# Perceiver block on one core: deviations of the projections' heads, centring of the keys' weights, scaling of inputs, and gathering of the lanes' maxima

## The chip, the cores and the metric

The kernel runs on one core of a Trainium2 chip. The metric is device time in microseconds (us) of one execution, and the median over runs is compared. The engines that matter are TensorE (PE: matmuls and transposes; PEld: its weight loads), VectorE (DVE), ScalarE (ACT), GpSimd (POOL), and the DMA queue of SyncE (SP), on which all transfers are issued. Each engine works through its own instruction list in order and waits for others by semaphores.

## The reference

A perceiver block, in float32, on x (128 x 512) and a context of 12,544 tokens of 512 channels. What matters for the change:

```python
def _ln(x, w, b):            # over the last axis
    mu = jnp.mean(x, -1); var = jnp.mean((x - mu)**2, -1)
    return (x - mu) * rsqrt(var + EPS) * w + b
def _div_clamp_fp8(x, scale):
    y = clip(x / scale, -448, 448)
    return fp8_roundtrip(bfloat16(y))
def _fp8_linear(x, wq, w_scale, in_scale):
    return (_div_clamp_fp8(x, in_scale) * in_scale) @ wq.T * w_scale
```

- x is normalised per row (`_ln`, the kernel does it twice in one), then four fp8-rounded projections give 16 query heads for the context (wqx), 8 key heads (wk), 8 value heads (wv) and 16 query heads for self-attention (wq), all of 128 channels, each with its own per-channel in_scale. The heads of wqx, wk and wq are layer-normalised per head.
- Self-attention over the 128 rows, and cross-attention of the same rows over the keys and values that w_kv_x makes from the context; its keys are layer-normalised per head too. Two heads of queries share a head of keys. Both results are fp8-rounded, projected and added to x.
- A causal 16-head attention with its projections, and a mixture of 32 experts of which each row takes 8.

## The kernel before, in words

**Stages.** (1) Norm of x, and twelve projections of 512 columns, each with 1 MB of weights; (2) self-attention in four groups of four heads; (3) cross-attention over 25 chunks of the context, 24 of 512 tokens and, as number 12 in the middle, one of 256 (the half chunk); (4) the causal attention and the experts.

**First stage (main loop L518 to L568).** `begin(name)` issues the four matmuls of a projection (shown as eight in the trace, ps_p, L462); weights come from a ring of three tiles w, and each begin loads the next. Projections run three ahead of their ends. `end(i)` (L477) normalises the four heads of projection i: `norm_heads` (L146) takes statistics on DVE (L152, L154), makes the variance plus eps (L156), its power of -1/2 (L158) and the weights' scale (L159) on POOL and minus mean times that, nb4b, on DVE (L161); ACT then writes the normalised pnn in four instructions (L163). PE turns pnn around (ps_t, L222), and ACT applies gain and bias (L474). Projections 6 and 7, the values, take one ACT copy instead. `quantised` (L444) divides the normalised x by in_scale (L192, four instructions of 128x128), rounds it (L198: a bfloat16 clip, a mask and additions) and multiplies by in_scale again (L448, four instructions); it runs once for each of the four projection kinds, on DVE.

**Keys and values of the context.** Each pair of key heads or of token blocks is made by a seven-product scheme (`unit`, L289; `k_unit` L321, `v_unit` L341): sums of weight blocks (`mix_weights`, wsum and wkv) and of context blocks (`mix_tokens`, L267 to L270, mix and ctx) are multiplied into three PSUM tiles a_ps, b_ps and c_ps, which DVE and ACT combine into KT and V through the copies p1, u2, u3 (u, L299). The keys' weights are first centred per head: a row sum on DVE (wm, L554), its scaling (L555), and its addition on POOL (L557), for eight blocks. In the first stage the units of chunk 0 fill PE between projections.

**A chunk.** `scores` (L639) multiplies KT with the queries and evicts with krs (the keys' 1/deviation, from `k_sums`, and from `k_rstd` with its matmul v_ps, kve and a power on POOL, L384); DVE takes block maxima mxr (L658). `max_rows` (L666) turns these into running maxima for two pairs of key heads at a time: a maximum over the chunk's token blocks (L673, 128 lanes), four copies of 32 lanes each into one tile of 32 lanes (L680), four reduces from it back to the four groups of 32 lanes (L686), and small additions (L691 to L699). `spread` (L713) subtracts the maximum (L725, DVE), exponentiates (L729, ACT), scales the running sums ol by al (L731, POOL) and adds the probabilities' sums to them (L739, POOL). `outputs` (L742) multiplies with V and adds to ol (L752). The loop over key heads g (L798 to L825) runs the values' units; the loop `keys` (L395) makes the keys of the next chunk between the outputs.

**Order.** The order on each engine is fixed when the program is built, by a scheduler that simulates durations; `tc.issue_after(x)` holds instructions back until x has been placed, and `tc.high_priority()` prefers them. So an edit can move neighbours. The lines that the change touches are in `norm_heads`, `norm_rows`, `quantise`, `quantised`, `end`, the main loop, `keys`, `max_rows` and the chunk loop.

Of the kernel before, what the change touches and what calls it, by code (L numbers as in the profile page):

```python
# [45 lines left out]
def block_kernel(  # L46
# [60 lines left out]
    nc.gpsimd.memset(ones, 1.0)  # L107

    fold = keep.tile([P, 32], F32, name="fold")
    nc.vector.tensor_tensor(fold, ident[:, 0:32], ident[:, 32:64], ALU.add)  # L110
    nc.vector.tensor_tensor(fold, fold, ident[:, 64:96], ALU.add)
    nc.vector.tensor_tensor(fold, fold, ident[:, 96:128], ALU.add)
    nc.vector.tensor_scalar(fold, fold, 1.0 / D, None, ALU.mult)
    rcol = keep.tile([P, NCOL], F32, name="rcol")
    c0 = _COLS["q_in"][0]
    nc.vector.reciprocal(rcol[:, c0 : c0 + 16], colt[:, c0 : c0 + 16])
    c1 = _COLS["smooth"][0]
    nc.vector.reciprocal(rcol[:, c1 : c1 + 32], colt[:, c1 : c1 + 32])

    qxT = keep.tile([P, NH, S], F32, name="qxT")  # L120

    qb = keep.tile([P, NH, 4], F32, name="qb")
    ps2 = keep.tile([P, 1], F32, name="ps2")
    nc.vector.tensor_tensor(ps2, scl("pin"), scl("pw"), ALU.mult)
    sc2 = keep.tile([P, 6], F32, name="sc2")
    nc.vector.tensor_tensor(sc2, sc, sc, ALU.mult)

# [18 lines left out]
    def norm_heads(dst, src, sname):  # L146


        st = small.tile([P, 4, 6], F32, tag="st4", name="st4")
        mv = small.tile([P, 4, 2], F32, tag="mv4", name="mv4")  # L150
        for j in range(4):
            nc.vector.bn_stats(st[:, j, :], src[:, j * D : (j + 1) * D])  # L152
        for j in range(4):
            nc.vector.bn_aggr(mv[:, j, :], st[:, j, :])  # L154
        v = small.tile([P, 4], F32, tag="ve4", name="ve4")
        nc.gpsimd.tensor_scalar(v, mv[:, :, 1], sc2[:, scn(sname)], EPS, ALU.mult, ALU.add)  # L156
        r = small.tile([P, 4], F32, tag="rs4", name="rs4")
        nc.gpsimd.tensor_tensor(r, v, mhalf[:, :4], ALU.pow)  # L158
        pool = nc.gpsimd.tensor_scalar(r, r, scl(sname), None, ALU.mult)  # L159
        b = small.tile([P, 4], F32, tag="nb4b", name="nb4b")  # L160
        dve = nc.vector.scalar_tensor_tensor(b, mv[:, :, 0], -1.0, r, ALU.mult, ALU.mult)  # L161
        for j in range(4):
            nc.scalar.activation(  # L163
                dst[:, j * D : (j + 1) * D], src[:, j * D : (j + 1) * D], AF.Identity,
                bias=b[:, j : j + 1], scale=r[:, j : j + 1],
            )
        return pool.ins, dve.ins

    def norm_rows(dst, src, twice=False):

        st = small.tile([P, 6], F32, tag="st1", name="st1")
        mv = small.tile([P, 2], F32, tag="mv1", name="mv1")
        nc.vector.bn_stats(st, src)
        nc.vector.bn_aggr(mv, st)


        v = small.tile([P, 1], F32, tag="ve1", name="ve1")
        if twice:
            nc.gpsimd.tensor_scalar(v, mv[:, 1:2], 1.0 + EPS, EPS * EPS, ALU.mult, ALU.add)
        else:  # L180
            nc.gpsimd.tensor_scalar(v, mv[:, 1:2], EPS, None, ALU.add)
        rs = small.tile([P, 1], F32, tag="rs1", name="rs1")
        nc.gpsimd.tensor_tensor(rs, v, mhalf[:, :1], ALU.pow)
        nc.vector.tensor_scalar(dst, src, mv[:, 0:1], rs, ALU.subtract, ALU.mult)

    def quantise(pool, dst, src, rname, k0):


        r0 = _COLS[rname][0] + k0
        t = pool.tile([P, 4, S], F32, tag="qz_t", name="qz_t")  # L190
        for k in range(4):
            nc.vector.tensor_scalar(  # L192
                t[:, k, :], src[:, k, :], rcol[:, r0 + k : r0 + k + 1], FP8_MAX,
                ALU.mult, ALU.min,
            )
        rounded(pool, dst, [t])
# [39 lines left out]
    V = vp.tile([P, CH // P, G * D], F32, name="V")  # L236
    rstds = {}

# [156 lines left out]
    def keys(c, others, pool, tag, todo=None, done=0):  # L395

        sums = {}
        todo = todo or parts(k_unit(c, u) for u in range(2))
        for i in range(done, 8):
            next(todo)  # L400
            if i % 4 == 3:
                sums[i // 4] = k_sums(c, i // 4)
            if others:
                others(i)
            if i == 6:
                k_rstd(c, 0, sums.pop(0), pool, tag)
        return sums

    with tc.tile_pool(name="pre", bufs=2) as pre, tc.tile_pool(name="pre1", bufs=1) as pre1, tc.tile_pool(
# [25 lines left out]
        xn = pre.tile([S, H], F32, tag="xn", name="xn", bufs=1)  # L435
        norm_rows(xn, x1c, twice=True)
        ps = transposed(pps, xn)
# [6 lines left out]
        def quantised(nm):  # L444
            t = pre.tile([P, NK, S], F32, tag="xq", name=f"x_{nm}")
            quantise(pre, t, lnT, nm, 0)
            for k in range(NK):
                end = nc.vector.tensor_scalar(t[:, k, :], t[:, k, :], col(nm, k), None, ALU.mult)  # L448
            return t, end.ins
# [17 lines left out]

        def end_norm(i, sname, wname, bname, dstT):
            ps = begun[i][0]
            n = pre.tile([S, H], F32, tag="pnn", name="pnn")  # L470
            last = norm_heads(n, ps, sname)
            with tc.issue_after(begun[i + 2][1]) if i + 2 < len(begun) else nullcontext():
                pt = transposed(pps, n)
            nc.scalar.activation(dstT, pt, AF.Identity, bias=col(bname), scale=col(wname))  # L474
            return last

        def end(i):  # L477
            if i < 4:


                qraw = pre.tile([P, 4, S], F32, tag="qT", name="qraw", bufs=4)
                last = end_norm(i, "wqx", "qxln_w", "qxln_b", qraw)
                nc.vector.tensor_scalar(
                    qxT[:, 4 * i : 4 * i + 4, :], qraw, col("kxln_w"), None, ALU.mult
                )
                qraws.append(qraw)
                return last
            if i < 6:
                return end_norm(i, "wk", "kln_w", "kln_b", kT[:, 4 * i - 16 : 4 * i - 12, :])
            if i < 8:  # L490
                nc.scalar.activation(
                    vv[:, (i - 6) * H : (i - 5) * H], begun[i][0], AF.Copy, scale=scl("wv")
                )
                return None
            qTs.append(pre.tile([P, 4, S], F32, tag="qT", name="qT", bufs=4))
            return end_norm(i, "wq", "qln_w", "qln_b", qTs[-1])

# [20 lines left out]
        for i in range(12):  # L518
# [15 lines left out]
            if i == 5:  # L534
                with tc.issue_after(begun[8][1]):
                    for h in range(NH):
# [3 lines left out]
                        )  # L540
                qbw = pre1.tile([32, NH, 4], F32, name="qbw")
                for k in range(4):
                    nc.vector.tensor_copy(qbw[:, :, k], psb[32 * k : 32 * k + 32])
                for b in range(4):
                    nc.vector.tensor_copy(qb[32 * b : 32 * b + 32], qbw)
            if i in (2, 6):
# [3 lines left out]

            for j in {3: (0,), 4: (1,), 5: range(2, 8)}.get(i, ()):
                wk = wkv[:, j % 4, j // 4, :H].rearrange("p (g d) -> p g d", g=4)
                wm = small.tile([P, 4], F32, tag="wm", name="wm", bufs=8)
                nc.vector.tensor_reduce(wm, wk, AX.X, ALU.add)  # L554
                nc.vector.tensor_scalar(wm, wm, -1.0 / D, None, ALU.mult)  # L555
                with tc.issue_after(pooled):
                    nc.gpsimd.tensor_tensor(  # L557
                        wk, wk, wm[:, :, None].to_broadcast([P, 4, D]), ALU.add
                    )
            if i == 7:  # L560
                for k in range(2):
                    for step in mix_weights(nc.vector, slice(0, H), k):
                        step()
            if i == 8:
                first_keys = parts(k_unit(0, u) for u in range(2))
                with tc.issue_after(begun[11][1]):
                    next(first_keys)
        made = pooled  # L568

        def weights_of(i):  # L570
# [24 lines left out]
        def heads_of(i, pe):  # L595
# [15 lines left out]
            for k in range(4):  # L611
                nc.tensor.matmul(psx, lhsT=cq[:, k, :], rhs=w[:, k, :], start=k == 0, stop=k == 3)  # L612
            load_ahead()
# [52 lines left out]
    def max_rows(c, j0, n):  # L666
# [4 lines left out]
        g0 = j0 % 2 * 2  # L671
        r = tmp.tile([P, 4, HS // 32], F32, tag="mx2", name="mx2")[:, : 2 * n, :]
        nc.vector.tensor_reduce(  # L673
            r, mxr[j0 // 2][:, g0 : g0 + 2 * n, :nt, :].rearrange("p g t k -> p g k t"),
            AX.X, ALU.max,
        )

        w = tmp.tile([32, 4, 32], F32, tag="mx4", name="mx4")[:, :, : 16 * n]
        for b in range(4):
            nc.vector.tensor_copy(  # L680
                w[:, b, :], r[32 * b : 32 * b + 32].rearrange("p g k -> p (g k)")
            )
# [115 lines left out]
    for c in range(NCH):  # L798
# [4 lines left out]
        for g in range(G):  # L803
# [10 lines left out]
            if g == 2 and c + 1 < NCH:  # L814
                with tc.issue_after(made):
                    for step in mix_tokens(c + 1):
# [379 lines left out]
```

## Time and profile before

| | us |
|---|---|
| median of 3 runs (lowest, highest) | 2197.46 (2194.74, 2199.66) |
| the profiled execution's own time | 2197.58 |
| its span | 2195.8 |
| PE busy | 2158.6 (98%) |
| DVE, POOL, ACT busy | 1298.3, 1075.0, 900.3 |
| mean granted PE clock | 0.995 |
| L680, four copies: one copy min / median / max | 0.159 / 0.169 / 1.214 |
| L384 krs, mean of one | 2.859 |
| L731, L739 on POOL, mean of one | 1.280, 0.732 |

The span starts with the first and ends with the last recorded instruction; the execution's own time adds what lies around it (1.8 us). In the rows of a timeline the columns are the start, the busy length, engine, line, operation, output and inputs, shapes and how many instructions the row joins; in brackets stand the idle time ahead of it and what ended that. In the rows by stage the busy time of PE, PEld, DVE, ACT and POOL follow the stage's length, each with its number of instructions, and then the granted PE clock, the busy share of the DMA and GB/s. A wait's row gives the total, how often, and the longest.

### The profile page before, as it was taken

The page shows a single profiled execution, that of the slowest core. Times are in us where ns is not written, and L with a number is a line of the kernel's source. Part 1 is how long each engine was busy: PE and PEld are TensorE (multiplying, and loading weights), DVE is VectorE, ACT ScalarE, POOL GpSimd, SP SyncE. Part 2 cuts the span into 40 slices and gives each one's busy share as a digit, 9 for nine tenths or more (in the row PEclk, how much of TensorE's full clock was granted, in tenths as well). Part 3 has the DMA queues.
Part 4 walks back from the last instruction along what each step waited for, and adds up shares of the span by engine and source line. Part 5 has one row for each costly group of instructions (what it writes and reads, how often), then busy time and mean ns, then how long its engine had stood idle before and what let it go on. Part 6 is the DMA issues. An engine that isn't in the chain of part 4 may idle for free.

```text
span 2195.8 us, 23886 instructions
## 1 busy us (share of the span) xinstructions
PE 2158.6 (98%) x8700; PEld 1539.2 (70%) x8700; DVE 1298.3 (59%) x2410; ACT 900.3 (41%) x1686; POOL 1075.0 (49%) x1165
## 2 busy tenths in 40 slices
PE   7999999999999999999899999999999999999999
PEld 3667767766776777677667776776777677676654
DVE  7565764675566457557675576567556646757311
ACT  2443444454345444434354344345434444541211
POOL 2314644764564466457554574475457447534000
PEclk9999999999999999999999999999999999999999
DMA  8300000000000000000000000000000000007593
GB/s 296 124 26 1 20 20 1 20 20 0 20 20 20 1 20 20 0 10 20 20 20 0 20 20 20 1 19 20 1 20 19 20 1 20 0 1 264 192 284 118
DMA packets 71221, 95.48 MB, mean 43 GB/s; under 512 B 3136, under 2 KB 39488, under 8 KB 71104
## 3 DMA queue, kind: packets, MB, share of 16 engines
q1 hardware_dynamic: 71104, 93.97, 13.0%
q8 instruction: 68, 1.11, 0.2%
q14 instruction: 49, 0.40, 0.1%
HBM read 93.69 MB, written 0.26 MB: 43 GB/s over the span
## 4 chain that ended last, share of the span: by engine, by line
PE 91%; DVE 5%; POOL 2%; ACT 1%; issue 1%; SPq 0%; DMA 0%; POOLq 0%; ACTq 0%; DVEq 0%
PE a_ps L329 15%; PE o_ps L747 15%; PE s_ps L647 14%; PE a_ps L348 14%; PE c_ps L329 7%; PE c_ps L348 7%; PE gu_ps L1111 4%; PE b_ps L348 4%; PE b_ps L329 4%; PE moe_acc L1132 2%; PE ps_p L462 1%; PE ps_proj L857 1%; PE ps_core L612 1%; POOL ol L739 1%; DVE mxr L658 1%
## 5 line engine op out<-in xcount | busy, mean ns | idle before, releaser
L739 POOL TENSOR_TENSOR ol<-ol,s 128x256 f32<-128x256 f32 x764 | 553.1, 732 | 31.2
L652 ACT ACTIVATE s<-s_ps,krs 128x256 f32<-128x256 f32 x784 | 324.0, 471 | 190.5 <-PE s_ps L647 178.4
L384 POOL TENSOR_TENSOR krs<-kve,mhalf 128x16 f32<-128x16 f32 (+1 forms) x50 | 142.9, 2859 | 528.4 <-DVE kve L382 528.4
L731 POOL TENSOR_TENSOR ol<-ol,al 128x512 f32<-128x512 f32 x192 | 243.5, 1280 | 295.0 <-DVE al L708 295.0
L647 PE MATMUL s_ps<-qxT,KT 128*128 128x256 f32 x1568 | 373.2, 381 | 2.8 <-ACT s L652 2.1
L747 PE MATMUL o_ps<-s,V 128*128 128x256 f32 x1568 | 371.0, 379 | 0.3 <-DVE V L318 0.3
L647 PEld LDWEIGHTS s_ps<-qxT,KT 128*128 128x128 f32 x1568 | 295.6, 190 | 104.6 <-issue 68.2
L658 DVE TRANSPOSE_TENSOR_REDUCE mxr<-s 128x32 f32<-128x1024 f32 (+1 forms) x200 | 242.9, 1215 | 188.0 <-ACT s L652 185.0
L747 PEld LDWEIGHTS o_ps<-s,V 128*128 128x128 f32 x1568 | 297.0, 190 | 41.4 <-DVE V L318 1.1
L729 ACT ACTIVATE s<-s 128x1024 f32<-128x1024 f32 (+1 forms) x200 | 208.3, 1042 | 157.0 <-DVE s L725 153.4
L725 DVE TENSOR_TENSOR s<-s,b_ps 128x1024 f32<-128x1024 f32 (+1 forms) x200 | 231.5, 1169 | 0.0
L299 ACT COPY u<-a_ps 128x512 f32<-128x512 f32 (+1 forms) x198 | 114.3, 577 | 241.2 <-PE a_ps L329 196.1
L329 PE MATMUL a_ps<-ctx,wkv 128*128 128x256 f32 (+1 forms) x800 | 186.2, 375 | 0.6 <-POOL ol L731 0.6
L348 PE MATMUL a_ps<-wkv,ctx 128*128 128x512 f32 x392 | 186.2, 597 | 0.0
L752 DVE TENSOR_TENSOR ol<-ol,o_ps 128x256 f32<-128x256 f32 x192 | 80.0, 417 | 175.6 <-PE o_ps L747 164.7
L329 PEld LDWEIGHTS a_ps<-ctx,wkv 128*128 128x128 f32 x800 | 149.9, 190 | 31.0 <-issue 11.9
L365 DVE TRANSPOSE_TENSOR_REDUCE sqr<-sq 128x16 f32<-128x512 f32 (+1 forms) x200 | 128.1, 678 | 59.8 <-ACT sq L363 59.8
L363 ACT ACTIVATE sq<-KT 128x1024 f32<-128x1024 f32 (+1 forms) x100 | 104.1, 1041 | 137.0 <-DVE KT L318 93.1
L318 DVE TENSOR_TENSOR KT<-c_ps,u 128x512 f32<-128x512 f32 (+1 forms) x50 | 34.1, 681 | 146.4 <-PE c_ps L329 146.3
L348 PEld LDWEIGHTS a_ps<-wkv,ctx 128*128 128x128 f32 x392 | 74.9, 191 | 52.8 <-issue 47.3
L329 PE MATMUL a_ps<-mix,wkv 128*128 128x256 f32 (+1 forms) x400 | 98.8, 391 | 10.6 <-ACT u L299 7.1
L329 PE MATMUL c_ps<-ctx,wsum 128*128 128x256 f32 (+1 forms) x400 | 93.7, 377 | 0.0
(217 smaller groups left out, 2773.8 us busy)
## 6 DMA issues: line engine op xcount, KB each, us to landing
ctx<-in_ctxT SPq DMA_DIRECT2D x23, 1024.0 KB, 5.0
gu<-in_w SPq DMA_DIRECT2D x32, 384.0 KB, 4.7
gu<-in_v SPq DMA_DIRECT2D x32, 384.0 KB, 5.4
dn<-in_w SPq DMA_DIRECT2D x16, 768.0 KB, 4.6
w<-in_wprojT SPq DMA_DIRECT2D x8, 1024.0 KB, 5.6
w<-in_wqxT SPq DMA_DIRECT2D x4, 1024.0 KB, 9.6
w<-in_wqT SPq DMA_DIRECT2D x4, 1024.0 KB, 4.9
wkv<-in_wkvT SPq DMA_DIRECT2D x8, 256.0 KB, 7.3
```

The costliest lines, as they stand in the source:

```text
L329: nc.tensor.matmul(ps[:, j * h : (j + 1) * h], lhsT=w[:, k, (2 * u + j) * D : (2 * u + j + 1) * D], rhs=x[:, k, :], start=first and j == k ...
L348: last_mm[0] = nc.tensor.matmul(ps, lhsT=x[:, k, v * P : (v + 1) * P], rhs=w[:, k, H : 2 * H], start=first and k == 0, stop=k == 1, skip_g ...
L365: nc.vector.tensor_reduce(r[:, 2 * j + i, : n // 32], sq[:, i, :n].rearrange("p (b i) -> p b i", i=32), AX.X, ALU.add, apply_transpose=True,)
L384: nc.gpsimd.tensor_tensor(rs[:, :, :nt], ve[:, :, :nt], mhalf.rearrange("p (g t) -> p g t", g=4)[:, :, :nt], ALU.pow,)
L647: end = nc.tensor.matmul(ps[:, t - t0, :], lhsT=KT[:, g, t * P : (t + 1) * P], rhs=qxT[:, 2 * g : 2 * g + 2, :], start=True, stop=True,)
L652: nc.scalar.activation(s[:, t, :], ps[:, t - t0, :], AF.Copy, scale=rs[:, t : t + 1])
L658: nc.vector.tensor_reduce(mxr[g // 4][:, g % 4, :nt, :].rearrange("p t k -> p (t k)"), s[:, :nt, :].rearrange("p t (k i) -> p (t k) i", i=32),
L725: nc.vector.tensor_tensor(s[:, :nt, :], s[:, :nt, :], ps[:, a, None, :].to_broadcast([P, nt, HS]), ALU.subtract,)
L729: nc.scalar.activation(s[:, :nt, :], s[:, :nt, :], AF.Exp, scale=scale)
L731: nc.gpsimd.tensor_tensor(ol[g], ol[g], alb[:, a, None, :].to_broadcast([P, 2, HS]), ALU.mult)
L739: summed[0] = nc.gpsimd.tensor_tensor(ol[g][:, 1, :], first, s[:, t, :], ALU.add).ins
L747: end = nc.tensor.matmul(ps, lhsT=V[:, t, g * D : (g + 1) * D], rhs=s[:, t, :], start=t == 0, stop=t == nt - 1,)
```

## The change

1. Constants (reciprocals of in_scale, the fold matrix and others) are issued behind the first norm's xn instead of at the start. New ones: epss = EPS / scale², the scale's sign, and gains = sign times the norm's weight.
2. `norm_heads`: the scale is folded into eps (the variance plus EPS / scale²), so L159 goes; variance plus eps and minus the mean are made on DVE, and POOL makes the power and nb4b.
3. `quantise`: one instruction over 128x512 for four, without the clip's minimum, which `rounded` applies anyway.
4. `quantised`: the multiplication by in_scale becomes one POOL instruction over 128x512, except for wqx's input.
5. The keys' weights are centred from iterations 6 and 7 on instead of 3 to 5; their mixes come at 8 and 9 instead of 7; the first keys' unit at 9 instead of 8; the copies qbw and qb after the loop.
6. The first krs of chunk 0 is placed with high priority behind the third ps_core.
7. `max_rows`: four reduces of 32 lanes each replace L673 and the copies L680; they read 32 lanes and write to lanes 0 to 31.
8. `mix_tokens(c + 1)` is placed behind the last sum of ol issued before (`summed[0]`) instead of `made`, from chunk 1 on.

```diff
     def norm_heads(dst, src, sname):
...
-        nc.gpsimd.tensor_scalar(v, mv[:, :, 1], sc2[:, scn(sname)], EPS, ALU.mult, ALU.add)
+        nc.vector.tensor_scalar(v, mv[:, :, 1], epss[:, scn(sname)], None, ALU.add)
+        nm = small.tile([P, 4], F32, tag="nm4", name="nm4")
+        dve = nc.vector.tensor_scalar(nm, mv[:, :, 0], -1.0, None, ALU.mult)
         r = small.tile([P, 4], F32, tag="rs4", name="rs4")
         nc.gpsimd.tensor_tensor(r, v, mhalf[:, :4], ALU.pow)
-        pool = nc.gpsimd.tensor_scalar(r, r, scl(sname), None, ALU.mult)
         b = small.tile([P, 4], F32, tag="nb4b", name="nb4b")
-        dve = nc.vector.scalar_tensor_tensor(b, mv[:, :, 0], -1.0, r, ALU.mult, ALU.mult)
+        pool = nc.gpsimd.tensor_tensor(b, nm, r, ALU.mult)
...
     def quantise(pool, dst, src, rname, k0):
...
-        for k in range(4):
-            nc.vector.tensor_scalar(
-                t[:, k, :], src[:, k, :], rcol[:, r0 + k : r0 + k + 1], FP8_MAX,
-                ALU.mult, ALU.min,
-            )
+        nc.vector.tensor_tensor(
+            t, src, rcol[:, r0 : r0 + 4, None].to_broadcast([P, 4, S]), ALU.mult
+        )
...
-            if i == 6:
-                k_rstd(c, 0, sums.pop(0), pool, tag)
+            if i == (6 if others else 4):
+                with ExitStack() as first:
+                    if not others:
+                        first.enter_context(tc.high_priority())
+                        first.enter_context(tc.issue_after(cores[2]))
+                    k_rstd(c, 0, sums.pop(0), pool, tag)
...
-        norm_rows(xn, x1c, twice=True)
+        make_constants(norm_rows(xn, x1c, twice=True))
...
+            if nm == "qx_in":
+                for k in range(NK):
+                    end = nc.vector.tensor_scalar(t[:, k, :], t[:, k, :], col(nm, k), None, ALU.mult)
+            else:
+                c0 = _COLS[nm][0]
+                end = nc.gpsimd.tensor_tensor(
+                    t, t, colt[:, c0 : c0 + 4, None].to_broadcast([P, 4, S]), ALU.mult
+                )
...
-            for j in {3: (0,), 4: (1,), 5: range(2, 8)}.get(i, ()):
+            for j in {6: range(4), 7: range(4, 8)}.get(i, ()):
...
-                nc.vector.tensor_reduce(wm, wk, AX.X, ALU.add)
+                with tc.issue_after(normed):
+                    nc.vector.tensor_reduce(wm, wk, AX.X, ALU.add)
...
-            if i == 7:
-                for k in range(2):
-                    for step in mix_weights(nc.vector, slice(0, H), k):
+            if i in (8, 9):
+                with tc.issue_after(normed):
+                    for step in mix_weights(nc.vector, slice(0, H), i - 8):
                         step()
-            if i == 8:
+            if i == 9:
                 first_keys = parts(k_unit(0, u) for u in range(2))
...
     def max_rows(c, j0, n):
...
-        r = tmp.tile([P, 4, HS // 32], F32, tag="mx2", name="mx2")[:, : 2 * n, :]
-        nc.vector.tensor_reduce(
-            r, mxr[j0 // 2][:, g0 : g0 + 2 * n, :nt, :].rearrange("p g t k -> p g k t"),
-            AX.X, ALU.max,
-        )
         w = tmp.tile([32, 4, 32], F32, tag="mx4", name="mx4")[:, :, : 16 * n]
         for b in range(4):
-            nc.vector.tensor_copy(
-                w[:, b, :], r[32 * b : 32 * b + 32].rearrange("p g k -> p (g k)")
+            nc.vector.tensor_reduce(
+                w[:, b, :].rearrange("p (g k) -> p g k", g=2 * n),
+                mxr[j0 // 2][32 * b : 32 * b + 32, g0 : g0 + 2 * n, :nt, :].rearrange(
+                    "p g t k -> p g k t"
+                ),
+                AX.X, ALU.max,
             )
...
             if g == 2 and c + 1 < NCH:
-                with tc.issue_after(made):
+                with tc.issue_after(summed[0] if c else made):
                     for step in mix_tokens(c + 1):
```

Both programs hold the same matmuls. In the built program POOL's scalings of x_k, x_v and x_q stand between the norms, its eight additions to the keys' weights behind nb4b of the sixth norm, and in a later chunk its mixes behind the sums of ol; the v_ps of chunk 0's first keys stands within the fourth ps_core.

## The prediction

> **What bounds the kernel now.** I read the busy table first, then the waits of the tensor engine, then the same engine by stage, then its timeline around each wait.
>
> ```profile
> span 2195.8 us, 23886 instructions
> PE 2158.6 (98%) x8700; PEld 1539.2 (70%) x8700; DVE 1298.3 (59%) x2410; ACT 900.3 (41%) x1686; POOL 1075.0 (49%) x1165
> ```
>
> PE is busy for 98% of the span. The change leaves its matmuls alone, so it can only win back PE's idle time and whatever matmuls lose behind idle time. By stage (length, PE, PEld, DVE, ACT, POOL busy, clock, DMA share, GB/s):
>
> ```profile
> 0.00:21.60 21.60, 14.15 (x28) 6.13 (x28) 13.33 (x44) 2.07 (x3) 3.74 (x13) 1.00 0.91 323
> 21.60:186.00 164.40, 151.36 (x572) 97.20 (x573) 113.28 (x300) 66.69 (x151) 54.10 (x67) 0.97 0.32 107
> 186.00:2019.00 1833.00, 1824.90 (x7483) 1340.09 (x7482) 1130.43 (x1965) 804.04 (x1464) 1015.53 (x1082) 1.00 0.06 18
> 2019.00:2195.80 176.80, 168.15 (x620) 95.78 (x618) 41.23 (x103) 27.52 (x68) 1.59 (x4) 1.00 0.66 211
> ```
>
> The first 21.6 us are the DMA's (0.91 busy, first context and weights), and the last 176.8 us the change does not touch. It can reach only the idle 13.0 us of the second stage and 8.1 us of the third. The waits there, and the matmuls behind three of them:
>
> ```profile
> PE a_ps L329 <- ACT u L299: 7.1, 1, 7.1
> PE ps_t L222 <- ACT pnn L163: 3.6, 2, 3.0
> PE a_ps L329 <- POOL ol L739: 3.5, 1, 3.5
> PE ps_t L222 <- ACT qraw L474: 2.9, 1, 2.9
> ```
>
> ```profile
> 46.11 1.45 PE L222 MATMUL ps_t<-ident,pnn 128*128 128x128 f32 x4 [2.89 <-ACT qraw L474]
> 47.35 5.28 PE L462 MATMUL ps_p<-w,x_v_in 128*128 128x512 f32 x8
> 52.46 0.60 PE L222 MATMUL ps_t<-ident,pnn 128*128 128x128 f32 x4
> 52.90 3.60 PE L462 MATMUL ps_p<-w,x_v_in 128*128 128x512 f32 x8
> ```
>
> The same eight matmuls take 5.28 behind the gap and 3.60 without one; the clock row gives 0.86 for 40 to 50 us. So a gap costs its length plus a slow stretch. My list, idle + slow excess over the undisturbed form:
> (a) first stage: 0.65 at 37.1; 2.89 + 2.53 at 46.1; 2.99 + 2.48 at 59.5: 11.5.
> (b) first scores of chunk 0: 0.65 at 142.2 (DVE x1c) and 1.10 at 146.2 (ACT s, behind POOL's krs, 2.92 long): 1.8.
> (c) 163.8: 1.0 (ACT s behind the exponentials).
> (d) 180.1: 3.51 + 1.54: 5.1. The row names POOL ol; ACT's u (179.36 to 179.93) came last, behind the exponential of L729.
> (e) 1018.8: 0.6 (POOL ol L731); 1981.8: 0.3 (V).
> (f) half chunk, 1076.8: 7.06 + 2.43: 9.5.
> Together 29.7 us.
>
> **First stage (a), part by part.** PE stands in order behind ps_t, which needs pnn, which needs nb4b and the POOL chain before it. The timeline of POOL and DVE:
>
> ```profile
> 43.77 1.04 POOL L557 TENSOR_TENSOR wkv<-wkv,wm 128x512 f32<-128x512 f32 x1
> 43.84 0.99 DVE L161 SCALAR_TENSOR_TENSOR nb4b<-mv,rs 128x4 f32<-128x4 f32 x1 [1.28 <-POOL rs L159]
> ```
>
> DVE idles 1.28 for POOL and is then held 0.99 on a 128x4 operation that takes 0.16 where POOL rests (73.98). The chain per norm now: POOL 0.27 + 1.04 + 0.30, DVE 0.16 to 0.99: 1.8 to 2.6. After: DVE ve and nm (L555, the nearest form, starts the next 0.07 later: 0.14 for both), POOL pow 1.04, POOL b about 0.30: 1.5, and DVE no longer waits within it. DVE's own work ahead of the sixth norm falls by: six of the eight L554 with L555 (0.68 each) 4.1; three L448 groups (0.78) 2.3; three L192 groups of four (0.78) turned into one 128x512 of about 0.60, 0.5; held nb4b 1.8; together 8.7. It gains 0.8 (12 small operations). The two gaps are 2.89 and 2.99 and the first 0.65, so 7.9 of freed DVE time covers them. Without stalls PE asks for the fourth norm's transposes at about 42.1, the sixth's at 49.9; my walk has pnn there at 38 to 39 and 47 to 48. Pessimistic, with DVE held by POOL at each step, 41 to 42 and 51.
>
> What POOL gains here: three scalings of 128x512 (nearest row L557: 1.04 each), one before each second norm. If one sits ahead of a pow, that norm is 1.04 later; the 3 us of margin hide it. POOL's eight L557 (8.3 us) move behind the sixth norm, about 48 to 57, and the keys' weight mixes (eight of 0.60 on DVE) behind that, to about 65; their first reader is the keys' a_ps, after the twelfth projection at about 72. Cover 7 us; without it PE would wait one for one. The constants move behind xn, into the time when the DMA has everything waiting: nothing from either end, since ps_p(2) waits for w's landing anyway.
>
> Here a rule speaks. The Trainium skill, "TensorE: Matmul & The Clock Gate", section "HAM oscillation — how this bites in real kernels", warns of idle gaps over about 3.4 us. By it gaps of 2.89 and 2.99 cost their length, and this part gains 5.9 + 0.65. The rows above show slow matmuls behind them, so I take 11.5. The measurement decides. I leave 0.5 (0 to 4.5).
>
> **Heads and start of chunk 0 (b, c).** krs(0) at high priority behind the third ps_core brings its 2.9 us ahead of the scores, and v_ps with its 4 us of PE work moves too: both waits of (b) go. In return POOL's mix of chunk 1 (4 x 1.27 from about 75) now meets nb, rl and pe of the first heads on DVE: 0 to 2, I take 1.1. (c) stays: 1.0.
>
> **Lane maxima (L673, L680 become L704).** Rows of the tile mx (min/median/max ns):
>
> ```profile
> L680 DVE COPY mx<-mx x200: 159/169/1214, 154.2 to 1980.4; 32x32 f32<-32x32 f32 x100
> L686 DVE TENSOR_REDUCE m_new<-mx x200: 350/367/379, 155.0 to 1982.8; 32x32 f32<-32x128 f32 x100
> L673 DVE TENSOR_REDUCE mx<-mxr x50: 199/376/384, 153.3 to 1979.0; 128x32 f32<-128x128 f32 x48, 128x32 f32<-128x64 f32 x2
> ```
>
> Before, 0.376 + 4 copies: 0.72 in all where POOL is quiet, 1.60 typically, 3.25 to 3.32 at (d) and (f). After, four reduces of the form nearest to L686 (also 128 elements in a lane, 32 lanes): 4 x 0.37 = 1.5, in the half chunk (64 elements, L673's minimum 0.20) 0.8. In a quiet group (1.1 before) that is 0.4 longer; behind it DVE has V's copy L318, which is not urgent there. In a typical second group (1.98 before) it is 0.5 shorter, ahead of the L318 that ended at 554.3 while the matmuls that read it came at about 555.8 (the seventh and eighth of o_ps's eight from 554.54): slack 1.5. In the held ones: (d) 3.7 to 1.5, (f) 3.45 to 0.8.
>
> The second rule: the Trainium skill, "GPSIMD Engine Reference", "Key points", says that GpSimd shares SBUF interfaces with VectorE and that DVE instructions in a 2-port mode or with two SBUF inputs contend. It speaks against moving scalings to POOL, and the held nb4b agrees. But copies reach 1.214 while the reduce never leaves 0.350 to 0.379 over 200 instances at the same places. By the rule alone new reduces, with one input, go free; by the copies' row they'd cost 1.4. I take 0.37.
>
> (d): the chain copies, L686, adds, L725, exponential, u shortens by 2.2 less what its adds still meet of POOL; but the scores also come earlier by (b). I leave 2.9 (1 to 5). (f): the adds L691 to L699 took 0.34, 1.19, 0.65, 1.30 there against 0.18 each in the quiet group at 534. POOL is in its ol work until about 1070.4, so some stay held. Wait 7.06 to about 2.7 and slow matmuls 2.43 to 1.5: leaves 4.2 (1.4 to 7).
>
> **Mix behind the sums.** POOL's four mixes (5.1 us, at 559.45 now) go behind the ol sums of the same group, to about 573 to 578. The order of the two programs as built puts krs next on POOL; it comes at 584.75 and POOL idled 6.9 before it. The mix is read a chunk later, at about 633. So 55 us cover it and the sums of ol come 5 us earlier: (e) falls from 0.9 to 0.2.
>
> **Sum.** Left: 0.5 + 1.1 + 1.0 + 2.9 + 0.2 + 4.2 = 9.9. Gain 29.7 - 9.9 = 19.8. The profiled execution took 2197.58 by its own time (span 2195.8): 2177.8. The median of the runs is 2197.46, 0.1 lower, so 2178.
>
> **Rivals.**
> 1. The forecast, 2178: chance 0.57. For it: every wait named has DVE work of the removed kind ahead of it.
> 2. Contention stays: POOL's scalings and b hold DVE (as at 43.84) so that (a) keeps 4.5, (d) 5.1, (f) 7, and the heads 2.5: left 19.1, gain 10.6: 2187. For it: 1.2 on 128x4 operations beside L267 too. Against it: DVE no longer runs nb4b. 0.22.
> 3. All stalls but 3 us go: gain 26.7, 2171. Against it: the adds at 1070 are two-input operations beside POOL. 0.08.
> 4. Slower: the lane reduces, which read one set of 32 partitions and write another as the copies do, are held as these are. Held to a copy's 1.214 plus the reduce's 0.20 more, each is 1.41. A second group has 3.5 us for them (1.98 now and the slack of 1.5), so PE stalls once a reduce exceeds 0.88: 4 x 1.41 - 3.5 = 2.1 in each of 24 chunks, 51 us, against 12.5 from the rest ((a) 11, (b), (e)): 2236. The whole is slower than before from about 1.0 each. Against it: L686. 0.06.
> 5. It does not do what it says: gaps only move, as the next norm or the DMA of a weight is late right behind (wqT's pieces land 4.9 us after issue in the median, and the DMA was 0.68 busy from 40 to 50): 2195, within 0.2%. 0.07.
>
> **Numbers.** 0.2% (4.4 us) is about what a measurement of this kernel can tell from no change. Faster 0.57 + 0.22 + 0.08 = 0.87, same 0.07, slower 0.06. The range 2170 to 2190 takes in the first three, with the bounds of (a), (d) and (f).
>
> **What would show it.** Right: ps_t rows at about 42 to 50 without idle time and with 3.60 for eight matmuls; the granted clock of the second stage near 1.0; L704 at 0.37 with no long maximum; u at the half chunk with about 3 us of wait. Wrong: L704 means over 0.5; b or the scalings on POOL far over 1.04; a wait on wkv or V ahead of a_ps or o_ps in every chunk; a wait of the keys' a_ps for wsum near 72.

## The result, and the profile after

The changed kernel takes 2187.50 us in the median of 5 runs (2185.38 to 2187.91), the kernel before 2197.46 (5 runs, 2194.74 to 2202.72): a ratio of 0.9948 with the interval 0.9937 to 0.9959. The profiled execution took 2187.21 with a span of 2185.4: 10.4 us less by both. The forecast was 2178 with a range of 2170 to 2190, so half of the expected gain is missing.

The busy table of the changed kernel and its two middle stages, between the same boundaries as before:

```profile
span 2185.4 us, 23824 instructions
PE 2159.9 (99%) x8700; PEld 1530.6 (70%) x8700; DVE 1302.4 (60%) x2341; ACT 897.3 (41%) x1686; POOL 1081.3 (49%) x1158
```

```profile
21.60:186.00 164.40, 159.81 (x627) 107.14 (x628) 113.03 (x281) 69.95 (x155) 59.60 (x65) 0.98 0.31 108
186.00:2019.00 1833.00, 1827.90 (x7476) 1327.97 (x7475) 1138.01 (x1918) 798.79 (x1464) 1018.50 (x1081) 1.00 0.06 20
```

PE's idle time in the second stage fell from 13.0 to 4.6 us, in the third from 8.1 to 5.1. But PE's busy time, with the same matmuls and fewer slow ones behind waits, rose by 1.3 us. That is where to look: something is lost inside rows that count as busy. The waits that answer to those of before:

```profile
PE a_ps L341 <- ACT u L311: 3.5, 3, 2.2
PE s_ps L676 <- ACT s L681: 1.6, 2, 1.3
PE a_ps L341 <- POOL ol L759: 1.2, 1, 1.2
PE ps_t L234 <- DVE pe L618: 1.0, 1, 1.0
```

All three waits for pnn and qraw are gone and the long one of the half chunk is 2.2. Read by this view alone the change would have kept its promise. The loss shows only where the two traces are laid beside each other chunk by chunk. I took the start of the first block maximum (mxr) of each chunk from the timelines, and subtracted it from that of the kernel before:

| us earlier than before at the start of chunk | 1 | 12 (half) | 13 | 24 | one full chunk lasts |
|---|---|---|---|---|---|
| before | 0 | 0 | 0 | 0 | 76.61 |
| changed kernel | 11.9 | 6.8 | 13.7 | 9.1 | 77.01 |

The lead melts by 0.40 in nearly every full chunk (by 1.05 in chunk 11, which makes the keys of the half chunk): 5.1 from chunk 1 to 12 and 4.7 from 13 to 24, 9.7 in all. Most of it is lost at two matmul groups of a chunk. First the kernel before in chunk 6 (start, length, engine, line), then the changed one at the same work:

```profile
621.62 1.06 ACT L729 ACTIVATE s<-s 128x1024 f32<-128x1024 f32 x1 [0.53 <-DVE s L725]
623.30 0.58 ACT L299 COPY u<-a_ps 128x512 f32<-128x512 f32 x1
622.54 1.89 PE L647 MATMUL s_ps<-qxT,KT 128*128 128x256 f32 x8
624.27 1.88 PE L348 MATMUL a_ps<-wkv,mix 128*128 128x512 f32 x4
625.99 1.88 PE L348 MATMUL c_ps<-wsum,ctx 128*128 128x512 f32 x4
```

```profile
612.25 1.06 ACT L757 ACTIVATE s<-s 128x1024 f32<-128x1024 f32 x1 [0.53 <-DVE s L753]
613.93 0.58 ACT L311 COPY u<-a_ps 128x512 f32<-128x512 f32 x1
612.67 1.89 PE L676 MATMUL s_ps<-qxT,KT 128*128 128x256 f32 x8
614.57 0.30 PEld L360 LDWEIGHTS a_ps<-wkv,mix 128*128 128x128 f32 x2 [0.41 <-ACT u L311]
614.57 1.98 PE L360 MATMUL a_ps<-wkv,mix 128*128 128x512 f32 x4
616.39 1.88 PE L360 MATMUL c_ps<-wsum,ctx 128*128 128x512 f32 x4
```

The scores ahead of a_ps begin at 622.54 and 612.67, so a_ps follows after 1.73 and 1.90, and c_ps after 1.72 and 1.82: 0.17 + 0.10 = 0.27 us lost, with no idle bracket in PE's rows; it stands with the weight load, 0.41 for ACT's u. In the kernel before, the copy u ended 0.39 ahead of a_ps (623.88, 624.27); in the changed kernel the exponential ahead of it waits for DVE and the rows on ACT are half a microsecond later, counted from the scores. The keys' a_ps loses about 0.10 more (1.76 and 1.80 for 1.73 each). The DVE rows that start the first loss, kernel before and changed:

```profile
607.70 0.38 DVE L673 TENSOR_REDUCE mx<-mxr 128x32 f32<-128x128 f32 x1
608.11 0.72 DVE L680 COPY mx<-mx 32x32 f32<-32x32 f32 x4
608.87 1.51 DVE L686 TENSOR_REDUCE m_new<-mx 32x32 f32<-32x128 f32 x4
610.41 0.69 DVE L318 TENSOR_TENSOR V<-c_ps,u 128x512 f32<-128x512 f32 x1
```

```profile
597.83 1.50 DVE L704 TENSOR_REDUCE mx<-mxr 32x32 f32<-32x128 f32 x4
599.37 1.12 DVE L714 TENSOR_REDUCE m_new<-mx 32x32 f32<-32x128 f32 x3
600.52 0.69 DVE L330 TENSOR_TENSOR V<-c_ps,u 128x512 f32<-128x512 f32 x1
601.24 0.37 DVE L714 TENSOR_REDUCE m_new<-mx 32x32 f32<-32x128 f32 x1
```

The four lane reduces take 0.4 longer than reduce and copies did (1.54 with their gap for 1.13), and 0.1 goes to the addition into V, which now splits the second row of reduces. The 0.10 at the keys' a_ps comes by way of POOL: its sums of ol are later too and reach into the second group (to 621.73), beside its first small addition, which takes 0.65 for 0.19. Changed kernel, and the kernel of the first experiment below, in which this loss is gone:

```profile
621.13 0.65 DVE L719 TENSOR_TENSOR m_new<-m_new,qb 128x32 f32<-128x32 f32 x1
```

```profile
616.86 0.19 DVE L731 TENSOR_TENSOR m_new<-m_new,qb 128x32 f32<-128x32 f32 x1
```

In the half chunk the same reduces pay. Kernel before, then changed:

```profile
1064.81 3.25 DVE L680 COPY mx<-mx 32x32 f32<-32x32 f32 x4
1076.84 3.75 PE L329 MATMUL a_ps<-mix,wkv 128*128 128x256 f32 x8 [7.06 <-ACT u L299]
```

```profile
1057.04 0.86 DVE L704 TENSOR_REDUCE mx<-mxr 32x32 f32<-32x64 f32 x4
1059.81 0.35 DVE L719 TENSOR_TENSOR m_new<-m_new,qb 128x32 f32<-128x32 f32 x1
1060.20 0.65 DVE L721 TENSOR_TENSOR m_new<-m_new 128x32 f32<-128x32 f32 x1
1065.44 1.96 PE L341 MATMUL a_ps<-mix,wkv 128*128 128x256 f32 x8 [2.24 <-ACT u L311]
```

The first stage runs without a wait in PE's rows from 26 to 85 us, but with one slow stretch that has no gap ahead of it:

```profile
51.36 3.60 PE L484 MATMUL ps_p<-w,x_q_in 128*128 128x512 f32 x8
54.80 4.61 PE L561 MATMUL ps_b<-colt,qraw 128*128 128x1 f32 x32
59.27 6.04 PE L484 MATMUL ps_p<-w,x_q_in 128*128 128x512 f32 x8
```

The granted clock from 54.8 to 65.2 us was 0.67; PE was busy in all 10.40 of these.

### The profile page after: what moved, and what is told of

It is laid out like the page before. It is cut to its first block, busy times and chain, and to the rows that moved or that the text cites. A ratio compares the mean times of both kernels' runs of the same rounds, so it can differ in the third digit from the quotient of the medians.

```text
span 2185.4 us, 23824 instructions
## 1 busy us (share of the span) xinstructions
PE 2159.9 (99%) x8700; PEld 1530.6 (70%) x8700; DVE 1302.4 (60%) x2341; ACT 897.3 (41%) x1686; POOL 1081.3 (49%) x1158
## 4 chain that ended last, share of the span: by engine, by line
PE 91%; DVE 4%; ACT 2%; DMA 1%; SPq 1%; issue 1%; POOL 0%; POOLq 0%; ACTq 0%; DVEq 0%
PE a_ps L341 15%; PE a_ps L360 15%; PE o_ps L775 14%; PE s_ps L676 14%; PE c_ps L341 7%; PE c_ps L360 7%; PE gu_ps L1139 4%; PE b_ps L360 4%; PE b_ps L341 4%; PE moe_acc L1160 2%; PE ps_p L484 2%; DVE s L753 1%; DVE mxr L687 1%; PE ps_core L638 1%; ACT s L681 1%; PE ps_proj L885 1%
## 5 line engine op out<-in xcount | busy, mean ns | idle before, releaser
L753 DVE TENSOR_TENSOR s<-s,b_ps 128x1024 f32<-128x1024 f32 (+1 forms) x200 | 230.2, 1170 | 0.0
L360 PE MATMUL a_ps<-wkv,mix 128*128 128x512 f32 x196 | 94.6, 605 | 0.0
```

Of the source, the lines that this page charges most:

```text
L360: last_mm[0] = nc.tensor.matmul(ps, lhsT=x[:, k, v * P : (v + 1) * P], rhs=w[:, k, H : 2 * H], start=first and k == 0, stop=k == 1, skip_g ...
L753: nc.vector.tensor_tensor(s[:, :nt, :], s[:, :nt, :], ps[:, a, None, :].to_broadcast([P, nt, HS]), ALU.subtract,)
```

## Experiments

My theory A after the result: the first group's lane reduces end later than reduce and copies did, and ACT passes that on to PE. Rival B: the mixes, moved behind the sums of ol, change what DVE meets on POOL. Four kernels tell them apart. Each ratio is to runs of the kernel before taken beside it, whose medians were 2197.7 to 2198.3.

**First group gathered by copies again.**

```diff
+        if j0 == 0:
+            r = tmp.tile([P, 4, HS // 32], F32, tag="mx2", name="mx2")[:, : 2 * n, :]
...
+            for b in range(4):
+                nc.vector.tensor_copy(
+                    w[:, b, :], r[32 * b : 32 * b + 32].rearrange("p g k -> p (g k)")
+                )
+        else:
+            for b in range(4):
...
-        for b in range(4):
```

> The changed kernel, but the first of the two max_rows groups of each chunk (j0 = 0) gathers its maxima as before, by one reduce and four copies; the second group keeps the four lane reduces. Theory A (each chunk of the changed kernel lasts 0.40 us longer because the lane reduces of the first group end 0.4 us later than reduce and copies did, and ACT's copy u and the a_ps behind it are late by that): the loss per chunk goes, a chunk lasts 76.58 again, time 2187.5 - 9.4 = about 2178 (2176 to 2181). Theory B (the 0.40 come from the mixes moved behind the sums of ol, which changes what DVE's additions meet on POOL): no change, 2187 to 2189, chunk 76.98.

Measured 2176.74 (ratio 0.9906, 0.9893 to 0.992). A chunk lasts 76.61. Theory A holds to about a microsecond, B falls. At chunk 24 the lead is 9.4 larger than in the changed kernel: 9.8 in the full chunks and 1.7 ahead of chunk 1, less 2.1 in the half chunk. The chain in chunk 6 of this kernel:

```profile
608.00 1.06 ACT L769 ACTIVATE s<-s 128x1024 f32<-128x1024 f32 x1 [0.53 <-DVE s L765]
609.68 0.58 ACT L311 COPY u<-a_ps 128x512 f32<-128x512 f32 x1
610.67 1.88 PE L360 MATMUL a_ps<-wkv,mix 128*128 128x512 f32 x4
612.39 1.88 PE L360 MATMUL c_ps<-wsum,ctx 128*128 128x512 f32 x4
```

The copy u ends at 610.26, 0.41 ahead of a_ps again.

**Both groups by copies** (part 7 undone).

```diff
+        r = tmp.tile([P, 4, HS // 32], F32, tag="mx2", name="mx2")[:, : 2 * n, :]
...
+            nc.vector.tensor_copy(
+                w[:, b, :], r[32 * b : 32 * b + 32].rearrange("p g k -> p (g k)")
-            nc.vector.tensor_reduce(
-                w[:, b, :].rearrange("p (g k) -> p g k", g=2 * n),
...
```

> The changed kernel with both groups gathered by reduce and copies as before (the change's part 7 undone alone). Theory A: the 0.40 per chunk goes or falls to at most 0.1; the half chunk's wait returns from 2.2 to 5 to 7 us with slow matmuls behind it, and the last wait of chunk 0 by about 2: 2180 to 2185. Theory B: the 0.40 stay and the half chunk's wait comes on top: 2191 to 2195.

Measured 2182.18 (0.993, 0.9916 to 0.9943), 76.61 per chunk; the half chunk waits 5.26 and its two matmul groups lose 2.0. As A had it, but for the last wait of chunk 0, which is 1.32 and not 2 longer than the 1.15 of the changed kernel.

**Mixes where they were** (part 8 undone).

```diff
-                with tc.issue_after(summed[0] if c else made):
+                with tc.issue_after(made):
```

> The changed kernel with the context's mixes placed as before (part 8 undone alone); PE, DVE and ACT have the same order as in the changed kernel. Theory A: the 0.27 us at the values' a_ps stays in each chunk, the 0.10 at the keys' a_ps may go either way: 2186 to 2190. Theory B: 76.58 per chunk, 2178 to 2180.

Measured 2192.76 (0.9979, 0.9971 to 0.9986), outside both. A chunk lasts 77.05, so B is wrong on the chunks; but without the moved mixes the half chunk's wait is 4.67 with a slow stretch of 2.3 instead of 2.24 with 0.1. I had not expected the mix to be worth that much there. With the mixes between POOL's sums of ol, the four small two-input operations behind the lane reduces take 4.4 us in all:

```profile
1060.28 1.21 DVE L719 TENSOR_TENSOR m_new<-m_new,qb 128x32 f32<-128x32 f32 x1
1061.52 1.19 DVE L721 TENSOR_TENSOR m_new<-m_new 128x32 f32<-128x32 f32 x1
1062.74 1.19 DVE L723 TENSOR_TENSOR sh<-m_new,qb 128x32 f32<-128x32 f32 x1
1063.85 0.76 DVE L727 TENSOR_TENSOR als<-m_new 128x32 f32<-128x32 f32 x1
```

In the changed kernel the same four took 1.9.

**The lane reduces alone, on the kernel before** (the reverse of the last diff, on that kernel).

> The kernel before with the four lane reduces alone (part 7 alone). Theory A: 0.27 to 0.40 more in each of 24 chunks (+6.5 to +9.6), half chunk about -6.5, end of chunk 0 about -2: 2195 to 2199, that is no gain at all although it takes away the longest wait. Theory B: only gains, 2189 to 2191.

Measured 2204.20 (1.0034, 1.0022 to 1.0045): slower than before, more than A said, since the half chunk gained only 1.6 and not 6.5. The part of the change with the most visible wait to remove loses by itself.

The same column as above for these and for three kernels below:

| us earlier at the start of chunk | 1 | 12 (half) | 13 | 24 | one full chunk |
|---|---|---|---|---|---|
| first group by copies | 13.6 | 13.6 | 18.4 | 18.5 | 76.61 |
| both by copies | 13.2 | 12.8 | 15.5 | 15.5 | 76.61 |
| mixes at made | 11.7 | 6.7 | 8.6 | 3.8 | 77.05 |
| before + lane reduces | 1.4 | -3.3 | -1.7 | -6.5 | 77.03 |
| parts 1 to 6 only | 9.7 | 9.8 | 9.5 | 9.5 | 76.61 |
| first by copies, norm as before | 7.1 | 7.1 | 10.7 | 10.8 | 76.61 |
| best (last below) | 15.9 | 15.9 | 22.8 | 22.9 | 76.61 |

In the half chunk (column 13 less column 12) the lane reduces alone bring 1.6, the moved mixes alone 2.7, both 6.9. One reason is in the rows behind the wait: slow matmuls of 2.0 to 2.7 follow waits of 4.7 to 7.1 in every profile, 1.8 to 3.1 follow waits of 3.25 to 3.32 in six, and about 0.1 follows a wait of 2.2 in two of three (1.8 in the third).

**The slow stretch behind ps_b.**

```diff
-            if i == 5:
-                with tc.issue_after(begun[8][1]):
-                    for h in range(NH):
+            if 3 <= i < 7:
+                with tc.issue_after(begun[i + 3][1]):
+                    for h in range(4 * i - 12, 4 * i - 8):
```

> The kernel of the first experiment (first group by copies) with the 16 products of one column each (ps_b, in one block of 3.6 us behind the ninth projection) placed four at a time behind the seventh to the tenth projection. In all profiles with the changed first stage the projection behind that block takes 5.38 to 6.04 us instead of 3.60 although PE had no idle time before it. Theory A (the block itself, 3.6 us of matmuls of one column, lets the clock drop): the projection falls to 3.60, ps_b stays 3.6 in sum, 2176.7 - 1.8 = about 2175. Theory B (the slow stretch has another cause, tied to time or to transfers): it stays somewhere near 56 to 64 us, 2176 to 2178.

Measured 2176.45 (0.9904, 0.9889 to 0.992): by the median 0.3, within the spread of the runs, so a shorter time is not shown. The profiled span is 2.3 shorter, 1.8 of it by the projection and 0.5 by a shorter wait for the weights of wk (0.36 for 0.84). Its trace decides for A, and so does that of the last kernel, whose rows are:

```profile
51.88 0.95 PE L561 MATMUL ps_b<-colt,qraw 128*128 128x1 f32 x8
52.69 0.64 PE L234 MATMUL ps_t<-ident,pnn 128*128 128x128 f32 x4
53.16 3.60 PE L484 MATMUL ps_p<-w,x_q_in 128*128 128x512 f32 x8
56.60 0.95 PE L561 MATMUL ps_b<-colt,qraw 128*128 128x1 f32 x8
57.41 3.68 PE L484 MATMUL ps_p<-w,x_q_in 128*128 128x512 f32 x8
```

No projection behind a part exceeds 3.7, while in all ten profiles with the changed first stage and ps_b in one block the next one took 5.37 to 6.59.

**Constants at the start** (part 1 undone, on the first experiment's kernel).

```diff
-        make_constants(norm_rows(xn, x1c, twice=True))
+        norm_rows(xn, x1c, twice=True)
...
+    make_constants(None)
+
     def stream_of(pool, stream):
```

> The kernel of the first experiment with the constants issued at the start, as before (part 1 undone alone). In the profiles the third projection starts at 21.60 and 21.73 with constants first and at 22.50 to 22.73 with constants behind xn. Theory A (the place of the constants moves the transfers' end): third projection back at about 21.7, time 0.9 lower, 2176. Theory B (the start does not depend on them; another difference of the two programs, or of the runs): third projection at 22.5 to 22.7, time unchanged within 0.5.

Measured 2178.34 (0.9914, 0.99 to 0.9927); third projection at 22.34. B: the place of the constants does not move the end of the transfers, and the time is not parted from the first experiment's (0.9893 to 0.992).

**Centring early** (part 5 undone, on the same).

```diff
-            for j in {6: range(4), 7: range(4, 8)}.get(i, ()):
+            for j in {3: (0,), 4: (1,), 5: range(2, 8)}.get(i, ()):
...
-            if i in (8, 9):
+            if i == 7:
...
-            if i == 9:
+            if i == 8:
```

> The kernel of the first experiment with the keys' weights centred from iterations 3 to 5 and their mixes at 7, the keys' unit at 8, as before (part 5 undone alone, its copies qbw and qb left behind the loop). Theory A (the six row sums, 4.1 us of DVE ahead of the sixth norm, with POOL's additions beside it, were the larger part of what the norms waited for): at least the wait of about 3 us at the transposes near 50 to 60 us returns with slow matmuls, 2176.7 + 4 to 8: 2181 to 2185. Theory B (the norm's own chain and the scalings were what mattered): within 1.5 of 2176.7.

Measured 2181.95 (0.9922, 0.9908 to 0.9936; runs from 2175.81 to 2182.47). One wait of 1.71 returns at the transposes at 53.4, ps_b and its projection are slow (4.09 and 6.59). A by its median, with a smaller wait than I said. The lead at chunk 1 is 2.5 smaller; the intervals overlap, so the time itself shows less than the trace.

**Lane reduces for both groups of the half chunk** (on the same).

```diff
-        if j0 == 0:
+        if j0 == 0 and nt > 2:
```

> The kernel of the first experiment, but in the half chunk both groups take the lane reduces (there each has 64 elements a lane, 0.19 us). Theory A (there the lane reduces are the shorter form, 0.8 against 0.2 + 4 copies, and each us of chain is a us of PE): the half chunk gains 1.6 more, as in the changed kernel (6.5 against 4.9), 2175. Theory B (the second group sets it alone): 2176.7 unchanged.

Measured 2176.81 (0.9907, 0.9893 to 0.992). The wait fell from 3.26 to 2.22, but in this profile 1.8 us of slow matmuls followed it. Inconclusive alone.

**Only parts 1 to 6** (the edits of the second and the third experiment together).

> The changed kernel with parts 7 and 8 undone: only the first stage and krs of chunk 0 (parts 1 to 6). Theory A (nothing in the chunks depends on these parts): 76.6 per chunk, half chunk's wait of 7 us as in the kernel before, the whole gain is what stands at the start of chunk 1 in the profiles with the changed first stage and copies, 13.2 to 13.6: 2184 to 2185. Theory B (the slower chunks come in part from the new first stage, or the mixes and maxima share in the gain there): off that by 2 or more.

Measured 2188.01 (0.9953, 0.9939 to 0.9966). Chunks of 76.61 and a half chunk with 7.06, as A said; but the lead is 9.7 and not 13.2, because the wait at the end of chunk 0 is back at 3.53 with slow matmuls of 1.8. That wait is cured by the mixes (1.32 with them moved and both groups by copies) and the maxima (0.66 in the first experiment), not by the first stage. So theory B was right in its second half, and my reading in A was wrong.

**Norm as before** (part 2 undone, on the first experiment's kernel).

```diff
-        nc.vector.tensor_scalar(v, mv[:, :, 1], epss[:, scn(sname)], None, ALU.add)
...
+        nc.gpsimd.tensor_scalar(v, mv[:, :, 1], sc2[:, scn(sname)], EPS, ALU.mult, ALU.add)
...
+        pool = nc.gpsimd.tensor_scalar(r, r, scl(sname), None, ALU.mult)
...
-        pool = nc.gpsimd.tensor_tensor(b, nm, r, ALU.mult)
+        dve = nc.vector.scalar_tensor_tensor(b, mv[:, :, 0], -1.0, r, ALU.mult, ALU.mult)
```

> The kernel of the first experiment with norm_heads as before: variance, power and scale on POOL, nb4b on DVE, gains without the sign (part 2 undone; one tiny copy on DVE more). Theory A (DVE's idle 1.3 us and its held nb4b per norm were a large part of the gaps): waits of 1 to 3 us return at the transposes between 40 and 60 us, 2179 to 2184. Theory B (the moved centring alone covers the gaps, and its L557 no longer holds nb4b): no wait there, 2176 to 2178.

Measured 2186.27 (0.9943, 0.993 to 0.9955): 9.5 more than 2176.74 (7.7 by the spans). Of these, 6.5 stand at chunk 1 (waits of 0.83 and 1.67 at the transposes, two of 0.5 to 0.6 at 85, ps_b and its projection slow at 4.37 and 6.30), and 1.2 at the half chunk, where the slow stretch may differ by chance. So of the parts of the first stage that were undone singly, the norm's chain is worth most; parts 3 and 6 were not undone singly. The rows show where it lies:

```profile
52.05 0.30 POOL L173 TENSOR_SCALAR rs<-rs,sc 128x4 f32<-128x4 f32 x1
52.39 0.16 DVE L175 SCALAR_TENSOR_TENSOR nb4b<-mv,rs 128x4 f32<-128x4 f32 x1 [1.53 <-POOL rs L173]
```

Here nb4b is not held (0.16; in the kernel before 0.99 in three norms, with L557 beside it at 43.84), but DVE still idles 1.5 for POOL.

**Scaling on DVE** (part 4 undone, on the same).

```diff
-            if nm == "qx_in":
+            if nm:
```

> The kernel of the first experiment with the multiplication by in_scale on DVE in four instructions for all four inputs (part 4 undone). Theory A (0.78 of DVE work per input is covered by the margin of about 2 us that the other parts leave): 2176 to 2177.5. Theory B (it is the part that keeps DVE ahead, or POOL's form holds DVE): 2 or more off, to either side.

Measured 2179.07 (0.9915, 0.9901 to 0.9928). The profile has no wait there and a lead at chunk 1 that is 0.2 smaller. The time is above A's range, the intervals overlap; I call it no difference that was shown.

**Split ps_b and the half chunk together** (both edits on the first experiment's kernel).

> Both additions together on the kernel of the first experiment: ps_b in four parts, and lane reduces for both groups of the half chunk. If both gains of the profiles add (2.3 for ps_b, 0.4 for the half chunk): 2174 to 2175.5. If the clock's slow stretch only moves: 2176 to 2177.

Measured 2174.32 (0.9894, 0.988 to 0.9907), the lowest median of all: 23 us less than before, 13 less than the changed kernel. Its interval overlaps that of the first experiment's kernel; the profile has no slow stretch behind ps_b and 0.1 behind the half chunk's wait of 2.26.

## Why the prediction was right and where it was wrong

The range and the sign held; the mechanisms of the likeliest case were right and one step failed, which took half the gain. That the time still lies in the range is in part luck: its width was drawn for (a), (d) and (f), not for a loss in each chunk. By the leads the changed kernel had 11.9 at chunk 1 (my steps gave 13.9), lost 9.7 in the full chunks (I gave 0.7 won at (e)), won 6.9 at the half chunk (5.3) and 1.3 behind the start of chunk 24 (nothing): 10.4 in place of 19.8. The time looks like rival 2's 2187, but not for its reason. By my steps:

- **First stage (a): right.** I left 0.5 of 11.5. The waits are all gone and the eight matmuls take 3.60, so by the rows (with the slow matmuls behind each gap) 11.5 came back. Two things I had not in the sum were taken off: the third projection starts 1.0 later (21.60 to 22.59), and ps_b's block costs 3.4 (1.0 + 2.4). The lead at the keys' a_ps is 7.3 (83.58 to 76.33). From ve to the end of nb4b the first six norms took 1.6 to 2.5 us, not 1.5 (the power took 1.39 in the median, for the 1.04 I used), and the margin bore it. I took the row sums for the largest item; with each part undone alone the lead at chunk 1 falls by 6.5 for the norm's chain and by 2.5 for the centring.
- **Heads and chunk 0 (b, c): right in size.** 0.99 for pe and 1.26 for ACT s, for 1.1 and 1.0.
- **End of chunk 0 (d): better than said.** Left 1.2 for 2.9. It had cost 5.3 and not 5.1, as c_ps behind a_ps lost 0.26 too, which my list left out.
- **Lane maxima: the duration was right, the cover was wrong.** I said 4 x 0.37 = 1.5 and L704 has 0.364 in the median and 0.377 at most: rival 4's held reduces did not occur.

```profile
L704 DVE TENSOR_REDUCE mx<-mxr x200: 188/364/377, 143.5 to 1971.6; 32x32 f32<-32x128 f32 x96, 32x32 f32<-32x64 f32 x4
```

  The step that failed is "that is 0.4 longer; behind it DVE has V's copy L318, which is not urgent there" (L318 is an addition into V). I costed it at nothing by naming the next instruction on DVE. Behind that stand L753, the exponential on ACT, and on ACT in order the copy u, for which PE's next a_ps had 0.39 us to spare. 0.4 plus 0.1 of a shift in order overran it by 0.27, and with the 0.10 at the keys' a_ps this came back in every full chunk. Rival 4 looked for a loss in each chunk, but from held reduces and at V's matmul in the second group, where there was none.
- **Mix behind the sums: larger than said.** I gave it 0.7 at (e), where the wait rose from 0.56 to 1.25. That is the lane reduces' doing: it is 0.50 with the first group by copies, and 0.56 with both, so the mixes changed little there. Undone alone it costs 5.3 us (2192.76 to 2187.50), nearly all of it in the half chunk.
- **Half chunk (f): right in direction, better in size.** Left 2.2 + 0.1, and a new wait of 0.4 at the scores, for 4.2. It took maxima and mix together.
- **The two rules.** By the rows a gap of 2.9 us is followed by a slow stretch; with both gaps gone the matmuls behind them take 3.60 again, so costing by the rows was right here. The rule of the Trainium skill ("GPSIMD Engine Reference", "Key points") on two inputs fits L719 and L721 (0.35 and 0.65 in the half chunk beside POOL, 0.19 in a quiet chunk) and the reduce with its one input, which is never held. Two things it leaves over: L723, with two inputs too, took 0.19 beside the same sums, and the copies, with one input, reached 1.214 before; whether they run in a 2-port mode no run shows.

Open: why the third projection starts at 22.3 to 22.7 in every kernel with the changed first stage, and at 21.6 to 21.7 in the two with the old one. The constants do not explain it, nor does the time of issue: its weights are issued at 9.3 to 9.7 us in all, but from 10 to 20 us the DMA moved 405 GB/s in those two and 380 to 383 in the twelve others. Why it is slower there stays open.

## What to carry to other kernels

A wait view can promise a gain and hide a loss: matmuls that each start 0.1 or 0.2 us late stay "busy", and repeated in every chunk 0.4 us outweighs the longest wait. So where an edit lengthens a chain in a loop, follow it through every engine's order to the next matmul, and write down the slack there in hundredths of a microsecond; the nearest instruction on the same engine is not the cover. Use the shorter form in each place: here copies where POOL was quiet, lane reduces where it was busy.

## What the runs showed of the hardware

- A block of 32 matmuls of one column, 3.6 to 4.6 us long, with PE busy just before and behind it, was followed by a projection of 5.4 to 6.6 us instead of 3.60, in ten profiles of ten (granted clock 0.67 from 54.8 to 65.2 us in the changed kernel's); in four parts of 0.95 us, with other matmuls between, it was not in either profile. In the two profiles of the old first stage, where a slow stretch had just ended, the block was followed by 3.68.
- After a wait of 2.2 us in the half chunk the next two groups, of the same instructions, were slow by 0.1 in two profiles and by 1.8 in a third; after 3.25 to 3.32 by 1.8 to 3.1 in six; after 4.7 to 7.1 by 2.0 to 2.7 in five. Elsewhere a wait of 2.52 (end of chunk 0, mixes at made) was followed by 0.1, one of 2.65 (first stage, the old one with lane reduces) by 2.4: the length of a wait does not tell the loss behind it.
- A reduce of 32x32 from 128 elements a lane that reads one group of 32 lanes and writes to another took 0.35 to 0.38 us in all 192 instances of the changed kernel, whatever POOL did beside it; copies of 32x32 took 0.159 to 1.214 in the kernel before.
